# Sums and combine weights spread over partitions by way of DRAM, and multiplied on GpSimd

## The chip, the cores and the metric

The kernel runs on one core of one Trainium2 chip. The metric is the device time of one execution in microseconds. Beside it stands a profile, which is one execution recorded by the hardware: PE is TensorE's matmul, PEld its weight load, DVE is VectorE, ACT is ScalarE, POOL is GpSimd, SP is SyncE, which only issues DMAs here. POOL can issue DMAs too. Each engine carries out its instructions in the order in which they were built.

## What is computed

The reference is eight layers in a row on x of (4, 512, 128): four attentions and four feed-forward parts in turn, each followed by a sum with its input and a layernorm. Two of the eight are touched. The seventh is attention with 16 heads of 64 in groups of 16 tokens with relative positions; its softmax divides by a sum of exponentials. The eighth is a mixture of 16 experts with gates and a shared expert:

```python
sim = einsum('bid,bjd->bij', q, k) * scale + einsum('btd,tsd->bts', q, k2) * scale
attn = softmax(sim, axis=-1)
out = einsum('bij,bjd->bid', attn, v) + einsum('bts,tsd->btd', attn, v2)
return out @ Wo.T + bo
...
weights, idx = _gate(x, w_gate)
combine = (one_hot(idx, E) * weights[..., None]).sum(1)
g = silu(einsum('th,efh->tef', x, w1_e)); u = einsum('th,efh->tef', x, w3_e)
routed = einsum('tef,ehf,te->th', g * u, w2_e, combine)
shared = _swiglu(x, w1_s, w3_s, w2_s)
```

The 16 heads' outputs have to be multiplied by 1/sum, and the hidden values of every expert by that token's combine weight.

## The kernel before

The tokens are four blocks ("batches" b = 0 to 3) of 512; block b lives in SBUF as X[b]. Eight stage objects run in the order Causal, F0, Rel, F1, Alibi, F2, A3, F3. A stage is written as Python generators that yield between small steps; `K.step` (L160) advances all generators of a list by one step, so their instructions are interleaved. A framework beneath then orders the instructions of each engine by priority and by its own estimates, inserts the waits, and that order is fixed in the program. `K.turn` (L175) gives out the banks of PSUM tag "b" in turn.

**A3**, the seventh layer (class at L1128), works in 32 units, t = 0 to 31: unit t is heads 2un and 2un+1 of block b, with b, un = divmod(t, 8). `prep` (L1283) makes queries and keys of the next unit and spreads them with DMAs, most of them from SP, two for each unit from POOL (L1312, a3KT<-H). `score` (L1327) makes 128 x 512 scores, their minimum on DVE (L1349) and the exponential on ACT with its sum (L1350, into den). `turn` (L1355) transposes the probabilities (L219 within `tr`), copies them to SBUF on ACT (L1363), and writes a band of them to DRAM (a3dpw) which is read back as `at` (L1376). `tail` (L1378) has two POOL instructions (L1386, L1387, from `at` to a2), 16 matmuls with the values (L1393), two more (L1406, L1407) and a copy to OT (L1409): two heads' outputs, one head on partitions 0 to 63, the other on 64 to 127, 512 tokens along the free axis.

After four units `fin` (L1414) ends one half (hf) of the heads of a block. It takes the reciprocal of the sums (L1422), splits it into a high and a low float32r part (L1423, L1424), transposes 4 x (128 x 16), copies to a3lT (L1430), and for each of the four OT runs a matmul with a table of ones, a3sel (L1436), that puts head 2pr's row on partitions 0 to 63 and head 2pr+1's on 64 to 127; DVE multiplies OT by that PSUM bank (L1437). Then 16 matmuls with Wo (L1447), a sum on DVE (L1449) and, after the second half, the layernorm. `fin` starts in `run` (L1459) at the units with t % 4 == 1; the last one starts after the loop and runs beside the beginning of F3.

**F3**, the eighth layer (class at L2180), first splits its weights into high and low parts, 18 pieces of 128 columns: DVE casts f3wh (L1935), POOL subtracts to f3wl (L1936). Then a loop over 36 steps (four blocks, nine of each: the shared expert and eight pairs of experts): `hidden` (L2268) has six matmuls of 128 x 512 (L313 to L315 within `mm3`), silu on ACT (L2277) and a product on DVE (L2279) that gives h. `gate` (L2203), a generator that is started `ahead` = 7 steps before its block's first, makes the combine weights: transposes of X, four matmuls (L2212), sigmoid (L2215), small DVE operations, comparisons in `rank` whose part on POOL is L1924 (eqf3g over groups, four; eqf3e over experts, four), sums on DVE (L1926, L1928), normalisation (L2253), the split (L2256, L2257), transposes and the copy to f3cT (L2265). `weigh` (L2282), `lag` = 4 steps behind `hidden`, has a matmul with a table of ones, f3sel (L2287), which spreads two experts' weights over 64 partitions each, and the multiplication on DVE (L2288). `out` (L2290), two steps behind that, has four matmuls (L2297); after eight pairs and the shared expert, a sum (L2302) and the layernorm. There are `lag` + 5 = 9 buffers for h.

Of the kernel before, what the change touches and what calls it, by code (L numbers as in the profile page):

```python
# [7 lines left out]
F32 = mybir.dt.float32  # L8
# [31 lines left out]
class K:  # L40
# [249 lines left out]
    def split_w(self, pool, src, n, name, scales=(), tag=None, raw=("wraw", 1)):  # L290

        nc = self.nc
        h = pool.tile([P, n], F32R, name=name + "h", tag=(tag or name) + "h")
        l = pool.tile([P, n], F32R, name=name + "l", tag=(tag or name) + "l")

        def fill():
            for s in range(0, n, 512):
                e = min(n, s + 512)
                w = pool.tile([P, 512], F32, tag=raw[0], name=f"wraw{self.next()}", bufs=raw[1])
                self.late(nc.sync.dma_start(w[:, :e - s], src[:, s:e]))  # L300
                yield
                yield
                for a, b, f in scales:
                    if a <= s < b:
                        nc.vector.tensor_scalar(w[:, :e - s], w[:, :e - s], f, None, ALU.mult)
                nc.vector.tensor_copy(h[:, s:e], w[:, :e - s])
                nc.gpsimd.tensor_tensor(l[:, s:e], w[:, :e - s], h[:, s:e].bitcast(F32), ALU.subtract)
                yield
        return h, l, fill()

    def mm3(self, out, wh, wl, xh, xl):
        nc = self.nc
# [800 lines left out]
def a3_constants():  # L1113
    c = {}
    ql = np.arange(P)[:, None]
    x = np.arange(512)[None, :]
    c["c_right"] = (x >= ql).astype(np.float32)
    st = np.zeros((32, 2, 2, T), np.float32)
    for bk in range(32):
        st[bk, :, :, 16 * bk + 32:] = 1.0  # L1120
    c["c_step"] = st.reshape(64, 2, T)
    r = np.arange(16)[None, :]
    c["c_d16"] = (r < 16 - ql % 16).astype(np.float32)
    c["c_sel3"] = heads(8)
    return c


class A3:  # L1128
# [93 lines left out]
    def operands(self):  # L1222
        k, nc, d, pool, w = self.k, self.nc, self.k.d, self.pool, self.w
        w["right"] = pool.tile([P, 512], BF16, name="a3right")
        nc.gpsimd.dma_start(w["right"], d["c_right"])
        w["sel"] = self.more.tile([P, 4, P], F32R, name="a3sel")
        self.lT = k.rows16(self.more, "a3lT")
        nc.gpsimd.dma_start(w["sel"], d["c_sel3"])

        self.QT, self.KT, self.Q2, self.K2 = ([pool.tile([P, 2, T], F32R, name=f"a3{n}{i}") for i in range(2)] for n in ("QT", "KT", "Q2", "K2"))  # L1230
        for i in range(2):
            nc.gpsimd.dma_start(self.K2[i][64:P], d["c_step"])
# [145 lines left out]
    def tail(self, t):  # L1378
# [32 lines left out]
        self.left -= 1  # L1411
        yield

    def fin(self, b, hf, X):  # L1414

        k, nc, w, pool = self.k, self.nc, self.w, self.pool
        u = k.next()
        den = self.S[b][2]
# [40 lines left out]
    def run(self, Xs):  # L1459
# [720 lines left out]
class F3:  # L2180
# [22 lines left out]
    def gate(self, b, X):  # L2203
# [57 lines left out]
        for c in range(4):  # L2261
            k.tr(ps[:32, c * P:(c + 1) * P], c2[:, c, :])
        yield
        cT = self.cTs[b % 2]
        nc.scalar.copy(cT[:32], ps[:32, :])  # L2265
        self.cT[b] = cT

    def hidden(self, b, j):  # L2268
        k, nc, w, pool = self.k, self.nc, self.w, self.pool
# [12 lines left out]
    def weigh(self, b, j, h):  # L2282
        k, nc, w = self.k, self.nc, self.w
        while b not in self.cT:
            k.step(self.gs)
        cb = k.bank("t")
        nc.tensor.matmul(cb, w["sel"][:, j, :], self.cT[b], start=True, stop=True)  # L2287
        nc.vector.tensor_tensor(h, h, cb, ALU.mult)  # L2288
# [19 lines left out]
    def run(self, Xs):  # L2308
# [1 line left out]
        self.w["2"] = k.load(pool, d["f3_w2"], [P, 9, P], "f3w2")  # L2310
        self.w["sel"] = pool.tile([P, 8, P], F32R, name="f3sel")
        nc.gpsimd.dma_start(self.w["sel"], d["c_sel"])
        self.cTs = [k.rows16(pool, f"f3cT{i}") for i in range(2)]
# [94 lines left out]
```

## Time and profile before

| what | value |
|---|---|
| median of 3 runs | 2244.88 us (2244.24 to 2246.5) |
| the profiled execution's own time | 2239.62 us |
| its span | 2237.9 us |
| granted TensorE clock, mean | 0.965 |
| POOL busy | 501.9 us |
| DMA moved | 242.10 MB, of it POOL's queue (q0) 17.50 MB |
| A3, from its first units to its last | about 1550 to 2107 us |
| F3, from its first matmul of `hidden` to the end | 2112 to 2238 us |

The 2237.9 us of the span are what the views cut up; the profiled execution took 1.7 us more than its span. The page gives busy time for each engine, the span in 40 slices of 56 us, and groups of instructions by line. A row of a group reads: line, engine, operation, out<-in, count, busy us and mean ns of one, then the idle time of the engine before them and what ended most of it. Times in rows of the timeline are start and duration in us; "[5.21 <-DMA f3w...]" at the end of one is the engine's idle time before it and what ended that. Line numbers are those of the kernel before.

### The profile page before, as it was taken

To read this page: it belongs to the slowest core of one execution; us is meant where nothing else is said; L and a number is where in the kernel's file an instruction comes from. 1 tells how busy PE (TensorE), PEld (TensorE's weight loads), DVE (VectorE), ACT (ScalarE), POOL (GpSimd) and SP (SyncE) were. 2 spreads that over 40 slices of the span, in tenths; PEclk is the share of its full clock that TensorE was granted. 3 is DMA by queue.
4 is the path that set the end of the run, shared out by engine and by line. 5 is a ranking of instruction groups with operands and counts; after the bars stand their busy time and mean duration, and the time that the engine had idled before them with its cause. 6 is when DMAs were issued, how large, how long until landed. Compare 5 with 4: busy or idle time off the path is not lost.

```text
span 2237.9 us, 43122 instructions
## 1 busy us (share of the span) xinstructions
PE 2025.4 (91%) x14400; PEld 1477.7 (66%) x14400; DVE 1664.1 (74%) x5592; ACT 1333.5 (60%) x2983; POOL 501.9 (22%) x706
## 2 busy tenths in 40 slices
PE   7999788888888999999999999998999999999897
PEld 4666566676665667676887665786666566666676
DVE  5778689888878677873777785544777877778787
ACT  3566787787734656665333666333777777767632
POOL 3222212111212532433000322531111111111220
PEclk9999999999978999999999999999999999999999
DMA  5321322021433454421021420604888878888400
GB/s 171 106 77 35 109 50 57 6 48 27 116 113 108 130 175 125 127 65 57 15 67 48 116 78 15 219 17 112 214 209 198 211 192 193 199 194 211 99 5 15
DMA packets 264918, 242.10 MB, mean 108 GB/s; under 512 B 106352, under 2 KB 190618, under 8 KB 263866
## 3 DMA queue, kind: packets, MB, share of 16 engines
q1 hardware_dynamic: 259146, 221.33, 37.2%
q0 software_dynamic: 5232, 17.50, 3.3%
q8 instruction: 115, 1.88, 0.3%
q14 instruction: 105, 0.86, 0.1%
q10 hardware_dynamic: 320, 0.52, 0.1%
HBM read 103.82 MB, written 74.32 MB: 80 GB/s over the span
## 4 chain that ended last, share of the span: by engine, by line
PE 59%; DVE 17%; ACT 10%; DMA 7%; issue 4%; POOL 2%; SPq 1%; ACTq 0%; POOLq 0%; DVEq 0%
PE t L219 5%; PE s L2129 4%; PE o L1393 3%; PE o L744 3%; PE s L695 3%; PE t L728 3%; PE o L1032 3%; PE b L313 3%; PE b L219 3%; PE o L2025 3%; DMA a3dpw<-p 2%; PE s L313 2%; PE b L315 2%; PE b L314 2%; PE s L315 2%
## 5 line engine op out<-in xcount | busy, mean ns | idle before, releaser
L985 DVE CUSTOM_DVE_ANT_0 junk<-w,a1mask 128x640 bf16<-128x640 f32 x256 | 203.1, 818 | 67.3 <-PE w L983 65.4
L219 PE MATMUL t<-ident,p 128*128 128x128 f32 x1280 | 201.9, 279 | 23.8 <-ACT p L1350 15.7
L772 ACT ACTIVATE Pt<-t 128x384 f32<-128x384 f32 (+1 forms) x384 | 179.5, 528 | 65.8 <-PE t L728 54.4
L219 PEld LDWEIGHTS t<-ident,p 128*128 128x128 f32 x1280 | 151.7, 142 | 81.0 <-ACT p L1350 39.0
L1363 ACT COPY PT<-t 128x512 f32<-128x512 f32 x256 | 149.9, 596 | 71.9 <-PE t L219 70.9
L1059 ACT ACTIVATE Pt<-t 128x512 f32<-128x512 f32 x256 | 149.1, 597 | 72.7 <-PE t L1058 44.5
L1350 ACT ACTIVATE p<-s,nb 128x512 f32<-128x512 f32 x256 | 178.6, 702 | 12.8 <-DVE nb L1349 8.4
L1349 DVE TENSOR_REDUCE nb<-s 128x1 f32<-128x512 f32 x256 | 175.0, 687 | 2.6
L1368 DVE CUSTOM_DVE_ANT_0 jk<-p,a3right 128x496 bf16<-128x496 f32 (+3 forms) x256 | 125.0, 488 | 29.2 <-ACT p L1350 17.8
L697 DVE CUSTOM_DVE_ANT_0 junk<-s,a0mask 128x128 bf16<-128x128 f32 (+3 forms) x256 | 114.2, 485 | 43.4 <-PE s L695 42.4
L697 DVE CUSTOM_DVE_ANT_0 junk<-s,a2mask 128x128 bf16<-128x128 f32 (+3 forms) x256 | 114.9, 484 | 28.3 <-PE s L695 27.9
L781 POOL TENSOR_SCALAR_AFFINE_SELECT Pt<-Pt 128x512 f32<-128x512 f32 x112 | 69.9, 636 | 249.0 <-ACT Pt L772 248.9
L1344 PE MATMUL s<-a3KT,a3QT 128*128 128x512 f32 x256 | 118.9, 465 | 7.3 <-DMA a3K<-L 4.1
L1347 DVE TENSOR_TENSOR s<-s,W 128x160 f32<-128x160 f32 (+1 forms) x256 | 81.1, 318 | 56.1 <-PE s L1345 55.2
L1393 PE MATMUL o<-PT,V 128*64 128x512 f32 x512 | 116.9, 599 | 0.5 <-ACT PT L1363 0.5
L1707 ACT ACTIVATE p<-sm,nb 128x128 f32<-128x128 f32 x256 | 100.6, 396 | 24.8 <-DVE nb L1705 24.3
L1345 PE MATMUL s<-a3K,a3Q 128*128 128x512 f32 x256 | 102.7, 401 | 0.1
L1705 DVE CUSTOM_DVE_ANT_0 sm<-s,band,rn 128x128 f32<-128x128 f32 x256 | 78.3, 344 | 26.5 <-PE s L1692 19.3
L1056 PE MATMUL t<-a1Q,a1K 128*128 128x512 f32 (+3 forms) x256 | 92.4, 366 | 6.2 <-ACT Pt L1059 3.6
L695 PE MATMUL s<-a0K,a0Q 128*128 128x256 f32 (+2 forms) x256 | 83.6, 387 | 14.0 <-DVE mx L697 6.8
L982 PE MATMUL w<-a1K,a1Q 128*128 128x256 f32 (+2 forms) x192 | 83.8, 437 | 9.3 <-DVE mx L985 8.3
L2012 ACT ACTIVATE sl<-s 128x512 f32<-128x512 f32 x64 | 38.0, 598 | 91.0 <-PE s L315 85.6
(494 smaller groups left out, 5812.7 us busy)
## 6 DMA issues: line engine op xcount, KB each, us to landing
W<-a3dsk SPq DMA_DIRECT2D x32, 640.0 KB
a1Q<-a1iq SPq DMA_DIRECT2D x32, 512.0 KB
a3dpw<-p SPq DMA_DIRECT2D x64, 160.0 KB
a3dpw<-p SPq DMA_DIRECT2D x64, 144.0 KB
a1K<-a1ik SPq DMA_DIRECT2D x64, 128.0 KB
a3Q<-a3dim SPq DMA_DIRECT2D x32, 256.0 KB
a3KT<-H POOLq DMA_DIRECT2D x64, 128.0 KB, 4.4
a3KT<-H SPq DMA_DIRECT2D x64, 128.0 KB
```

Of the source, the lines that this page charges most:

```text
L219: return self.nc.tensor.matmul(out.bitcast(x.dtype), x, i[:n, :n], is_transpose=True, start=start, stop=stop)
L695: self.scored = nc.tensor.matmul(s[:, :nm], self.qof(0, t, i)[:, qc * P:(qc + 1) * P], Ks[:, i, :nm], start=True, stop=True).ins
L697: nc.vector.tensor_tensor_reduce(junk[:, :n], s[:, :n], k.mask[:, 512 - n:512], 1.0, NEG, ALU.add, ALU.max, mx[:, qc, i:i + 1])
L772: ready = nc.scalar.activation(Pt[:, i, z:], s[:, z:], AF.Exp, scale=sc).ins
L985: nc.vector.tensor_tensor_reduce(junk, s.rearrange("p a n -> p (a n)")[:, T - n:T + m], k.mask[:, T - n:T + m], 1.0, NEG, ALU.add, ALU.max ...
L1059: nc.scalar.activation(Pt[:, i, :T], s, AF.Exp, scale=sc)
L1344: nc.tensor.matmul(s, QT[:, e, qs], KT[:, e, :], start=True, stop=False)
L1349: nc.vector.tensor_reduce(nb, s, AX.X, ALU.min)
L1350: nc.scalar.activation(p[:, e, :], s, AF.Exp, bias=nb, scale=-1.0, accum_out=den[:, qc, 2 * un + e:2 * un + e + 1])
L1363: self.copied[t] = nc.scalar.copy(PT[e][:, :, qc * P:qc * P + P], tb.rearrange("p (c n) -> p c n", n=P)).ins
L1368: nc.vector.tensor_tensor_reduce(jk[:, :nn], p[:, e, x0:], w["right"][:, :nn], 1.0, 0.0, ALU.mult, ALU.add, at[:, e, qc, 31:32])
L1393: m = nc.tensor.matmul(o[64 * e:64 * e + 64, :], V[:, kc, h * 64:h * 64 + 64], PT[e][:, kc, :], start=(kc == 0), stop=False)
```

## The change

In A3 the reciprocals are no longer split and spread by a matmul. A new generator `sums` takes the reciprocal, transposes it in float32, copies the 8 rows to SBUF and writes them to a DRAM tile with a DMA from POOL (`rows_out`). It starts three items into the fourth of four units (t % 4 == 0; after the last unit at its first item), so ahead of `fin`. `fin` reads two rows for each OT back with two DMAs from POOL, each of which sends one row of 512 values to 64 partitions (`rows_in`), and POOL multiplies OT by that. Two buffers alternate: one of the stage's own, and the one that the tile a3z had. `fin`'s matmuls with the table and its products on DVE go, as do the table a3sel and the tile a3lT.

In F3 block 0 stays as it was. For blocks 1 to 3 the gate transposes the weights in float32, copies 16 rows to SBUF, writes them to DRAM from POOL, and reads them back into two tiles of 128 x 4 x 512, each with two DMAs of 64 partitions; POOL multiplies h by a slice of these. The matmul with f3sel and DVE's multiplication go for these blocks.

```diff
+    def rows_out(self, rows, name):
+        n = rows.shape[0]
+        d = self.dr.tile([n, T], F32, tag=f"rows{n}", name=name, bufs=2)
+        self.nc.gpsimd.dma_start(d, rows)
+        return d
+
+    def rows_in(self, dst, d):
+        n = d.shape[0] // 2
+        for e in range(2):
+            ap = [[0, 64], [2 * T, n], [1, T]] if n > 1 else [[0, 64], [1, T]]
+            self.nc.gpsimd.dma_start(dst[64 * e:64 * e + 64], bass.AP(tensor=d.tensor, offset=d.offset + e * T, ap=ap))
...
@@ A3.operands @@
-        w["sel"] = self.more.tile([P, 4, P], F32R, name="a3sel")
-        self.lT = k.rows16(self.more, "a3lT")
-        nc.gpsimd.dma_start(w["sel"], d["c_sel3"])
...
+    def sums(self, b, hf):
+        k, nc = self.k, self.nc
+        u = k.next()
+        rd = self.more.tile([P, 4, 8], F32, tag="rd", name=f"rd{u}", bufs=2)
+        nc.vector.reciprocal(rd, self.S[b][2][:, :, 8 * hf:8 * hf + 8])
+        yield
+        ps = k.bank("b")
+        for c in range(4):
+            k.tr(ps[:8, c * P:(c + 1) * P], rd[:, c, :])
+        yield
+        lr = self.more.tile([8, T], F32, tag="lrow", name=f"lrow{u}", bufs=1)
+        nc.scalar.copy(lr, ps[:8, :])
+        yield
+        self.S["R", b, hf] = k.rows_out(lr, f"a3rows{u}")
+
     def fin(self, b, hf, X):
...
-        lr = self.more.tile([P, 4, 16], F32R, tag="lr", name=f"lr{u}", bufs=1)
-        rd = self.more.tile([P, 4, 8], F32, tag="rd", name=f"rd{u}", bufs=2)
-        nc.vector.reciprocal(rd, den[:, :, 8 * hf:8 * hf + 8])
-        nc.vector.tensor_copy(lr[:, :, 0:8], rd)
-        nc.vector.tensor_tensor(lr[:, :, 8:16], rd, lr[:, :, 0:8].bitcast(F32), ALU.subtract)
-        yield from wait()
-        ps = k.bank("b")
-        for c in range(4):
-            k.tr(ps[:16, c * P:(c + 1) * P], lr[:, c, :])
-        lT = self.lT
-        nc.scalar.copy(lT[:16], ps[:16, :])
+        rows, rbs = self.S["R", b, hf], []
+
+        def load(pr):
+            rbs.append((self.early, self.more)[pr % 2].tile([P, T], F32, tag=("a3z", "rb")[pr % 2], name=f"rb{u}{pr}", bufs=1))
+            k.rows_in(rbs[-1], rows[2 * pr:2 * pr + 2])
+
+        load(0)
+        load(1)
         yield
         for pr in range(4):
-            yield from wait()
-            ps = k.bank("b")
             OT = self.S["O", b, 4 * hf + pr]
-            nc.tensor.matmul(ps, w["sel"][:, pr, :], lT, start=True, stop=True)
-            nc.vector.tensor_tensor(OT, OT, ps, ALU.mult)
+            nc.gpsimd.tensor_tensor(OT, OT, rbs.pop(0), ALU.mult)
+            if pr < 2:
+                load(pr + 2)
             yield
...
@@ A3.run @@
+            if t >= 4 and t % 4 == 0:
+                sums = self.sums(*divmod((t - 4) // 4, 2))
...
+                if j == (self.la if t < n else 0) and t >= 4 and t % 4 == 0:
+                    gs.append(sums)
...
@@ F3.gate @@
+        if b:
+            yield
+            yield from k.turn()
+            ps = k.bank()
+            for c in range(4):
+                k.tr(ps[:16, c * P:(c + 1) * P], cw[:, c, :])
+            yield
+            cr = pool.tile([16, T], F32, tag="cr", name=f"cr{u}", bufs=2)
+            nc.scalar.copy(cr, ps[:16, :])
+            rows, cb = k.rows_out(cr, f"f3rows{b}"), []
+            for i in range(2):
+                cb.append(pool.tile([P, 4, T], F32, tag="cb", name=f"cb{u}{i}", bufs=3))
+                k.rows_in(cb[i], rows[8 * i:8 * i + 8])
+            self.cT[b] = cb
+            return
...
@@ F3.weigh @@
+        if b:
+            nc.gpsimd.tensor_tensor(h, h, self.cT[b][j // 4][:, j % 4, :], ALU.mult)
+            return
         cb = k.bank("t")
         nc.tensor.matmul(cb, w["sel"][:, j, :], self.cT[b], start=True, stop=True)
         nc.vector.tensor_tensor(h, h, cb, ALU.mult)
```

More of the change, by code (lines that the diff above doesn't have):

```diff
@@ L1123, in a3_constants @@
     c["c_d16"] = (r < 16 - ql % 16).astype(np.float32)
-    c["c_sel3"] = heads(8)
     return c
@@ L1417, in fin @@
         u = k.next()
-        den = self.S[b][2]
         wait = k.turn if b == NB - 1 and hf else lambda: ()
-        lr = self.more.tile([P, 4, 16], F32R, tag="lr", name=f"lr{u}", bufs=1)
-        rd = self.more.tile([P, 4, 8], F32, tag="rd", name=f"rd{u}", bufs=2)
-        nc.vector.reciprocal(rd, den[:, :, 8 * hf:8 * hf + 8])
-        nc.vector.tensor_copy(lr[:, :, 0:8], rd)
-        nc.vector.tensor_tensor(lr[:, :, 8:16], rd, lr[:, :, 0:8].bitcast(F32), ALU.subtract)
-        yield from wait()
-        ps = k.bank("b")
-        for c in range(4):
-            k.tr(ps[:16, c * P:(c + 1) * P], lr[:, c, :])
-        lT = self.lT
-        nc.scalar.copy(lT[:16], ps[:16, :])
+        rows, rbs = self.S["R", b, hf], []
[4 more added lines that the diff above has]
+        load(1)
         yield
         for pr in range(4):
-            yield from wait()
-            ps = k.bank("b")
             OT = self.S["O", b, 4 * hf + pr]
-            nc.tensor.matmul(ps, w["sel"][:, pr, :], lT, start=True, stop=True)
-            nc.vector.tensor_tensor(OT, OT, ps, ALU.mult)
+            nc.gpsimd.tensor_tensor(OT, OT, rbs.pop(0), ALU.mult)
+            if pr < 2:
+                load(pr + 2)
             yield
@@ L2263, in gate @@
         yield
-        cT = self.cTs[b % 2]
-        nc.scalar.copy(cT[:32], ps[:32, :])
-        self.cT[b] = cT
+        nc.scalar.copy(self.cT0[:32], ps[:32, :])
+        self.cT[b] = self.cT0
     def hidden(self, b, j):
@@ L2312, in run @@
         nc.gpsimd.dma_start(self.w["sel"], d["c_sel"])
-        self.cTs = [k.rows16(pool, f"f3cT{i}") for i in range(2)]
+        self.cT0 = k.rows16(pool, "f3cT0")
         gs = self.gs = [self.gate(0, Xs[0])]
```

## The prediction

> **What bounds the kernel.** First the page: busy times and slices.
>
> ```profile
> PE 2025.4 (91%) x14400; PEld 1477.7 (66%) x14400; DVE 1664.1 (74%) x5592; ACT 1333.5 (60%) x2983; POOL 501.9 (22%) x706
> ...
> DMA  5321322021433454421021420604888878888400
> ```
>
> POOL is nearly free over the whole span, and the DMA engines are fullest in slices 29 to 37, where A3 runs. F3 comes after, with the DMA engines empty. The two stages have different limits, so each is read by itself.
>
> A3, 1600 to 2100 us, who waited for whom (total us, times, longest):
>
> ```profile
> POOL a L1386 <- DMA at<-a3dpw: 159.1, 16, 16.7
> POOL a3KT L1312 <- ACT H L1307: 145.7, 28, 9.2
> ...
> PE s L1344 <- DMA a3K<-L: 4.1, 3, 1.7
> ```
>
> POOL stands idle; PE hardly waits for DMA. PE's share of windows of 100 us there is 89 to 96%, and dense rows start 0.23 us apart for a 512-column matmul. But the chain of waits runs through transfers too: in 1720 to 1860 "DMA a3dpw<-p" alone holds 11.9% of it, in 1860 to 2085 two transfers and SP's issues about 17%. So A3 is mostly PE, with DMA close behind at 84% of its engines.
>
> F3, cut where each batch's combine weights are ready (end of the copy at L2265: 2140.4, 2165.2, 2190.9, 2216.9):
>
> ```profile
> core 0: us, PE busy (x) PEld busy (x) DVE busy (x) ACT busy (x) POOL busy (x), PEclk, DMA share, GB/s
> 2113.30:2140.60 27.30, 22.90 (x120) 18.45 (x119) 24.32 (x84) 9.15 (x16) 8.29 (x17) 0.94 0.00 1
> 2140.60:2165.40 24.80, 23.52 (x146) 19.59 (x145) 20.48 (x66) 8.88 (x15) 5.53 (x8) 1.00 0.01 2
> 2165.40:2191.10 25.70, 24.52 (x150) 20.74 (x150) 22.48 (x81) 9.64 (x15) 5.43 (x8) 1.00 0.04 11
> 2191.10:2217.00 25.90, 24.31 (x145) 20.04 (x144) 22.16 (x81) 8.63 (x13) 5.45 (x8) 1.00 0.04 11
> 2217.00:2229.10 12.10, 10.64 (x72) 9.16 (x72) 8.45 (x24) 0.00 (x0) 0.00 (x0) 1.00 0.08 22
> ```
>
> PE's starts sum to only some 20 us a round (54 of 0.23, 36 of 0.11, 8 of 0.23, small ones); its busy column is filled by modelled ends. The round is one gate: PE issues the next batch's L2212 right behind the transposes of this one's weights, and then sigmoid, DVE, POOL's L1924, DVE, transposes and copy follow one another. In the round from 2190.9: group ranks leave POOL 7.3 us in, expert ranks start 4.4 later and take 4.6, DVE needs 8.0 more, transposes and copy 1.7. The last row is the tail: 12.2 us from the copy to the last sum's reader.
>
> **The change, part by part**, against the profiled execution (2239.62 us, span 2237.9; the runs' median of 2244.88 lies 5.3 above).
>
> *A3, removed.* 32 matmuls with the table (L1436): 32 x 0.23 = 7.4 us of PE; PE's idle time before them is 8.6 more at most (3.8 + 3.2 + 1.6 by that line's rows). On DVE 32 multiplications of 0.68 and 8 x (0.17 + 0.18) for the split, 24.6 us. Transposes and ACT's copy stay. Bounds: 0 (something else ends the waits) to -16.0. I take 70% of the PE time and half of the idle time: -9.5.
>
> *A3, added.* 72 POOL issues of 0.52 and 32 multiplications of 1.28 (rows below): 78 us spread over stretches where POOL idles, so nothing by themselves. The transfers are 8.4 MB more. At the stage's own 197 GB/s that is 42.6 us if DMA decides, nothing if hidden: bounds 0 and +42.6. With DMA and SP holding about 15% of the chain I take 0.15 x 42.6 = +6.4. POOL's order puts two to four a3KT issues (L1312) behind a multiplication that waits for its rows: write and read back, some 10 us once in four units. In the trace a3KT is issued more than half a unit before its unit (1674.65, 1686.64, 1702.28, a unit being 16 us), so I take nothing; without that cover it is up to 4 us, seven times. A3 in sum: -3.
>
> The trace shows all queues together at 84%, POOL's own with 6.1%, and not what happens when POOL's grows. The Trainium skill ("DMA: Bandwidth & Descriptors", section "Issuing engines are not separate DMA queues") says that DMAs of any issuing engine share the same 16 engines and interleave. By it the idle POOL queue buys no room: with the full +42.6 in place of +6.4 the forecast would be 36 us later.
>
> *Into F3.* The last four outputs of A3 now go through POOL, ahead of the work that opens F3. Before:
>
> ```profile
> 2107.34 0.56 POOL L2312 DMA_DIRECT2D f3sel<-in_c_sel_dram  x1
> 2107.89 1.00 POOL L272 MEMSET f3cT<- 128x512 f32 x2
> 2109.16 2.59 POOL L1936 TENSOR_TENSOR f3wl<-f3w,f3wh 128x128 fp32r<-128x128 f32 x6 [0.26 <-DVE f3wh L1935]
> ```
>
> After, POOL's order is: rows out, two a2 instructions, four rb issues, f3sel, two multiplications, four issues, memset, the third multiplication, six f3wl, four eqf3g with four f3wl between, the fourth multiplication, eight f3wl, four eqf3e. PE's order puts the matmuls with OT before the first one with f3wl. From 2107.4: four issues to 2109.6; rows landed 2.5 us on, products to 2113.6; issues to 2115.8; third product 2118.7; six f3wl at 0.43 to 2121.3; ranks and f3wl to 2124.1; fourth product 2125.4; eight f3wl 2128.9; four eqf3e of 1.14 to 2133.5. They ended at 2128.4 before. So +5; bounds +3 (DVE, 24.3 of 27.3 busy there, was late anyway) to +9 (the delay of the first f3wl).
>
> *The rounds.* Batch 0 keeps its matmul, so the first round stays. The rows with prices:
>
> ```profile
> L1441 POOL TENSOR_TENSOR r<-X,a3bo 128x512 f32<-128x512 f32 x4 | 5.1, 1276 | 11.9 <-DVE X L375 11.9
> L1924 POOL TENSOR_TENSOR eqf3e<-eqf3e,f3tri 128x256 f32<-128x256 f32 x16 | 17.1, 1092 | 18.9 <-DVE eqf3e L1923 13.4 <-issue 4.2 <-DVE rs L345 0.4
> L2288 DVE TENSOR_TENSOR h<-h,t x32: 669/682/690, 2141.9 to 2227.2; 128x512 f32<-128x512 f32 x32
> DMA to landing us min/median/max: 3.8/3.8/3.8
> ```
>
> The last is f3sel: 512 KB on quiet engines, of which 256 KB of output moved at about 300 GB/s in the same state; fixed part about 2.5. From the end of the copy: rows issued and landed +2.6; cb waits for that, four issues of 0.55; the first megabyte lands 5.5 after its first issue, +8.1 (bound above: f0v's 5.5 for 512 KB, twice, +13.6; below +7). POOL then runs in its written order: three multiplications mixed with eqf3g, four more, one eqf3e, the eighth, three eqf3e: 8 x 1.28 + 4 x 0.25 + 4 x 1.14 = 15.8, to +23.9. Before, eqf3e ended at +16.3. DVE's 8.0 afterwards shrinks by about three L2288 (2.0) and the dropped split (0.4): 5.6, then 1.7: a round of 31.2 against 25.9. As DVE also loses 5.5 us elsewhere in the round I take 30.5, +4.7 for each of the rounds 2 and 3: +9.4 (bounds +4 and +20).
>
> *The end.* Copy, +8.1, eight multiplications 10.2, last four matmuls and the wait 0.7: 19.0 instead of 12.2: +6.8 (bounds +5 and +12).
>
> DVE and POOL in one another's way: in the first gate DVE's L344, L346 and L349 take 0.73, 0.70 and 0.70 beside eqf3e instead of 0.16, and end with it; in later gates eqf3e runs beside DVE's 0.42 us rows unstretched. The Trainium skill ("Advanced Engine Details and Errata", section "VectorE Performance Modes") says that DVE's second SBUF port is shared with GpSimd, so two-port DVE instructions and POOL's block each other. Eight waits of 0.55 would fit in the 4 us in which eqf3e queues behind multiplications; by the page the sum may rise some 3 us, by the rows it does not.
>
> Sum: -3 + 5 + 9.4 + 6.8 = +18.2, 2257.8 for the profiled execution and 2263 for the median.
>
> **The rivals.** *Faster:* DVE decides the rounds (22.2 of 25.9 us busy). Freed of eight multiplications a round loses 5.5, and latency hides behind the nine h buffers: -11, A3 -14 with nothing lost to DMA, end +6.8: 2227. It decides when POOL reaches eqf3e before DVE has it ready, that is when the seventh multiplication ends less than 11.7 us into the round; with rows landing at +8.1 it ends near +18. Chance 0.13. *Level:* A3 gains its whole 16 and the three F3 terms sit at their lower bounds, 12: -4, about 2242 to 2247. Chance 0.13. *DMA or POOL decides A3:* the transfers come in lumps of 1 MB (5.3 us at 197 GB/s) in one unit of four, whose 16 us are 84% full already; a3Q, a3K and a3KT are late and A3 loses 30: 2296. For it the chain's transfers, against it PE's 7 us of waiting in all. Chance 0.14. *It does not do what it says:* excluded, the built order has 56 table matmuls fewer.
>
> **Numbers.** Forecast 0.60, its own range 2250 to 2280. Range for all 2241 to 2288: left out are the faster rival and the upper part of the DMA one. Faster by over 0.2% (about what a measurement of this kernel can tell from no change) 0.13, within 0.13, slower 0.74.
>
> **What would show it.** Right: copies of the weights about 30 us apart in rounds 2 and 3; eqf3e idle-free behind multiplications; some 19 us from the last copy to L2302; the first f3wl some 9 us later than in the row above; A3 within a few us of before. Wrong: rounds under 26 us, or a3KT and a3Q among PE's longest waits.

## The result and the profile after

The changed kernel takes 2322.0 us (median of 6, 2317.47 to 2331.26) against 2244.57 (median of 6): 1.0353 times, with a 95% interval of 1.0325 to 1.0381. It is slower, as predicted, but by 77 us, not 18, and outside the range. The profiled execution took 2317.61 us, its span is 2315.9, 78.0 longer than before. The page of the changed kernel, busy times and the DMA row of the slices:

```profile
PE 2038.6 (88%) x14344; PEld 1488.5 (64%) x14344; DVE 1665.6 (72%) x5514; ACT 1333.8 (58%) x2983; POOL 616.3 (27%) x846
...
DMA  5321411012326444212204206038899887887123
```

56 table matmuls are gone, POOL has 114 us more, and the span is longer although no engine but POOL is busy for a larger share of it. So most of the time went into waits. Where, is read from four marks: the first and the last copy to OT, the copies of the weights in F3, and the sum after the last block. Starts in both traces, differences worked out from them:

| stretch | before | after | difference | forecast |
|---|---|---|---|---|
| start to first copy to OT | 1586.6 | 1587.4 | +0.8 | 0 |
| A3: first to last copy to OT | 522.9 | 569.9 | +47.0 | -3 |
| last copy to OT to first copy of weights | 30.3 | 38.1 | +7.8 | +5 |
| first to second copy | 24.8 | 24.1 | -0.7 | 0 |
| second to third, third to fourth copy | 25.7, 26.0 | 32.4, 33.6 | +14.3 | +9.4 |
| last copy to last sum | 12.8 | 21.6 | +8.8 | +6.8 |

A3 alone holds 50 of the 60 us that the forecast lacks. Two rows of windows tell in what form: A3 before, then A3 after, each from its first copy to OT to just after its last.

```profile
core 0: us, PE busy (x) PEld busy (x) DVE busy (x) ACT busy (x) POOL busy (x), PEclk, DMA share, GB/s
1586.00:2110.00 524.00, 492.37 (x2753) 326.76 (x2752) 406.57 (x1179) 384.59 (x906) 72.06 (x128) 0.99 0.83 197
```

```profile
1587.00:2158.00 571.00, 503.23 (x2727) 336.28 (x2725) 401.34 (x1144) 385.33 (x909) 143.17 (x219) 0.95 0.82 193
```

PE is idle for 571.00 - 503.23 = 67.77 us where it was for 31.63: +36.1. And with fewer matmuls its busy time grows by 10.9, because the granted clock falls from 0.99 to 0.95. The DMA share is what it was. Before, PE's largest wait in A3 (1590 to 2110 us) was this, and none ahead of the matmuls with Wo (L1447) is in that answer:

```profile
PE t L219 <- ACT p L1350: 14.8, 23, 2.1
```

Who waited for whom in 1600 to 2150 us, after:

```profile
POOL a L1396 <- DMA at<-a3dpw: 132.1, 14, 13.4
POOL a3KT L1322 <- ACT H L1317: 107.1, 21, 8.5
...
POOL OT L1456 <- DMA rb<-a3rows: 47.1, 16, 4.9
PEld b L1468 <- POOL OT L1456: 40.7, 15, 6.9
PE b L1468 <- POOL OT L1456: 37.4, 13, 6.7
```

L1468 are the matmuls with Wo (L1447 before). They wait for POOL's multiplication, and that waits for the loaded rows; PE and its weight load show the same waits, so they are not added up. One half, on POOL:

```profile
1628.47 0.54 POOL L315 DMA_DIRECT2D a3rows<-lrow  x1
1631.16 2.07 POOL L323 DMA_DIRECT2D rb<-a3rows  x4 [2.15 <-DMA a3rows<-lrow]
1638.14 1.27 POOL L1456 TENSOR_TENSOR OT<-OT,rb 128x512 f32<-128x512 f32 x1 [4.91 <-DMA rb<-a3rows]
1639.71 1.07 POOL L323 DMA_DIRECT2D rb<-a3rows  x2 [0.30 <-POOL OT L1456]
...
1641.82 1.33 POOL L1456 TENSOR_TENSOR OT<-OT,rb 128x512 f32<-128x512 f32 x1
1644.63 1.28 POOL L1456 TENSOR_TENSOR OT<-OT,rb 128x512 f32<-128x512 f32 x1 [1.49 <-DMA rb<-a3rows]
1645.85 1.09 POOL L323 DMA_DIRECT2D rb<-a3rows  x2
...
1651.82 1.26 POOL L1456 TENSOR_TENSOR OT<-OT,rb 128x512 f32<-128x512 f32 x1 [3.68 <-DMA rb<-a3rows]
```

From the rows' DMA to the end of the fourth product 24.6 us pass: write 2.4, load, product, and with two buffers a second turn of load and product, of which the last load stands behind the third product. The transposes of the reciprocals had ended at 1626.51, so from there the chain is 26.6 us long; in the other halves it is 22 to 26. PE had 16.7 us of other work between these transposes and its first matmul with Wo (15 to 18 in seven of the eight halves, 7 in the last). It came to the matmul with the fourth OT at 1646.45, stood for 6.68 us, and went on at half speed:

```profile
1646.50:1649.00 2.50, 0.00 (x0) 0.00 (x0) 0.29 (x1) 0.00 (x0) 1.56 (x3) 1.00 1.09 248
1649.00:1653.00 4.00, 0.00 (x0) 0.00 (x0) 0.68 (x1) 1.72 (x4) 1.18 (x1) 0.56 1.04 230
1653.00:1656.00 3.00, 2.87 (x12) 2.68 (x12) 1.18 (x4) 0.00 (x0) 0.08 (x1) 0.50 0.05 14
1656.00:1660.00 4.00, 4.00 (x34) 3.78 (x32) 1.83 (x9) 3.78 (x10) 0.00 (x0) 0.96 0.00 0
```

The column before DMA's share is the granted clock: 1.00 until some 3 us into the wait, then 0.50 until some 3 us after PE is busy again. In the third row DMA is empty too: SP stood 7.4 us for ACT's p before it could issue the next transfers of a3dpw.

F3, windows cut at the end of the copies (the rows that answer to those shown of before):

```profile
2196.00:2220.10 24.10, 22.36 (x138) 19.19 (x137) 21.02 (x55) 9.21 (x14) 4.16 (x8) 1.00 0.00 1
2220.10:2252.50 32.40, 25.92 (x147) 22.16 (x145) 26.65 (x72) 9.75 (x16) 17.33 (x21) 0.89 0.34 75
2252.50:2286.10 33.60, 26.52 (x140) 21.98 (x139) 25.89 (x71) 8.74 (x13) 17.03 (x21) 0.85 0.33 72
2286.10:2307.10 21.00, 14.48 (x89) 13.03 (x88) 6.48 (x27) 1.80 (x3) 12.85 (x13) 0.84 0.52 115
```

Block 0 keeps its matmul, and its round is as before; the others are 7 and 8 us longer, with the clock at 0.89 and 0.85. The last row is the end.

### The profile page after: what moved, and what is told of

It is laid out like the page before. It is cut to its first block, busy times and chain, and to the rows that moved or that the text cites. A ratio compares the mean times of both kernels' runs of the same rounds, so it can differ in the third digit from the quotient of the medians.

```text
span 2315.9 us, 43157 instructions
## 1 busy us (share of the span) xinstructions
PE 2038.6 (88%) x14344; PEld 1488.5 (64%) x14344; DVE 1665.6 (72%) x5514; ACT 1333.8 (58%) x2983; POOL 616.3 (27%) x846
## 4 chain that ended last, share of the span: by engine, by line
PE 51%; DVE 17%; DMA 12%; ACT 10%; issue 5%; POOL 4%; SPq 1%; POOLq 0%; ACTq 0%; DVEq 0%
PE s L2154 4%; PE t L219 3%; DMA rb<-a3rows 3%; PE s L709 3%; PE o L758 3%; PE t L742 3%; PE o L1046 3%; PE b L219 2%; PE o L2050 2%; PE o L1403 2%; PE b L327 2%; PE s L327 2%; PE s L329 2%; PE s L328 2%; DVE junk L999 2%
## 5 line engine op out<-in xcount | busy, mean ns | idle before, releaser
L219 PE MATMUL t<-ident,p 128*128 128x128 f32 x1280 | 206.0, 283 | 18.4 <-ACT p L1360 10.2
L219 PEld LDWEIGHTS t<-ident,p 128*128 128x128 f32 x1280 | 156.6, 144 | 83.5 <-ACT p L1360 36.8
L1360 ACT ACTIVATE p<-s,nb 128x512 f32<-128x512 f32 x256 | 178.1, 700 | 20.6 <-DVE nb L1359 12.5
L1378 DVE CUSTOM_DVE_ANT_0 jk<-p,a3right 128x496 bf16<-128x496 f32 (+3 forms) x256 | 135.5, 529 | 29.6 <-ACT p L1360 18.7
L711 DVE CUSTOM_DVE_ANT_0 junk<-s,a0mask 128x128 bf16<-128x128 f32 (+3 forms) x256 | 114.1, 484 | 42.6 <-PE s L709 41.7
L1468 PE MATMUL b<-a3wo,OT 128*128 128x128 f32 x256 | 49.0, 330 | 47.9 <-POOL OT L1456 46.8
```

The source lines that it names most:

```text
L219: return self.nc.tensor.matmul(out.bitcast(x.dtype), x, i[:n, :n], is_transpose=True, start=start, stop=stop)
L711: nc.vector.tensor_tensor_reduce(junk[:, :n], s[:, :n], k.mask[:, 512 - n:512], 1.0, NEG, ALU.add, ALU.max, mx[:, qc, i:i + 1])
L1360: nc.scalar.activation(p[:, e, :], s, AF.Exp, bias=nb, scale=-1.0, accum_out=den[:, qc, 2 * un + e:2 * un + e + 1])
L1378: nc.vector.tensor_tensor_reduce(jk[:, :nn], p[:, e, x0:], w["right"][:, :nn], 1.0, 0.0, ALU.mult, ALU.add, at[:, e, qc, 31:32])
```

## The experiments

The theories: **W**, PE's written order puts the matmuls with Wo where the old path was through and the new one is not, so PE waits; **T**, my rival on record, the traffic of the loads; **P** or **M**, POOL's order and its multiplications. For F3: **D**, the trip through DRAM, against M. In the table A3 is the time from the first to the last copy to OT; the next column goes from there to the first copy of weights; rounds are first to last copy of weights, all three; the end is last copy to last sum. Ratios are those to the kernel before, run on the same chip, with 95% intervals.

| kernel | ratio | A3 | into F3 | rounds | end |
|---|---|---|---|---|---|
| before | 1 | 522.9 | 30.3 | 76.5 | 12.8 |
| after | 1.0353 (1.0325 to 1.0381) | 569.9 | 38.1 | 90.1 | 21.6 |
| e1_a3_part | 1.0265 (1.0224 to 1.0306) | 576.1 | 38.9 | 78.1 | 14.2 |
| e2_f3_part | 1.0092 (1.0063 to 1.0121) | 522.6 | 28.4 | 92.0 | 21.8 |
| e3_rows_unread | 1.0151 (1.0115 to 1.0188) | 558.7 | 35.0 | 76.4 | 12.9 |
| e4_wo_later | 1.0083 (1.0051 to 1.0115) | 531.6 | 37.3 | 78.7 | 12.5 |
| e5_wo_later_sp | 1.0267 (1.0235 to 1.0299) | 578.1 | 38.3 | 78.6 | 12.5 |
| e6_a3_dve | 1.0206 (1.0166 to 1.0247) | 562.6 | 36.1 | 77.4 | 12.6 |
| e7_f3_dve | 1.0120 (1.0081 to 1.0158) | 519.8 | 28.3 | 90.3 | 22.6 |
| e8_f3_bank_pool | 1.0049 (1.0030 to 1.0067) | 524.1 | 30.6 | 77.1 | 23.2 |
| e9_rows_unread_order | 1.0168 (1.0137 to 1.0200) | 545.1 | 39.4 | 77.8 | 12.8 |
| e10_wo_later_act | 1.0118 (1.0087 to 1.0150) | 540.5 | 37.2 | 78.6 | 12.5 |
| e11_spread | 1.0074 (1.0053 to 1.0095) | 526.0 | 38.0 | 75.8 | 12.8 |
| e12_loads_only | 1.0130 (1.0094 to 1.0165) | 551.0 | 34.4 | 76.1 | 12.8 |
| e13_small_loads | 1.0132 (1.0099 to 1.0165) | 549.1 | 38.1 | 76.2 | 12.8 |
| e14_small_loads_only | 0.9989 (0.9970 to 1.0008) | 522.7 | 33.1 | 76.1 | 12.7 |
| e15_spread_last | 1.0028 (1.0011 to 1.0044) | 530.8 | 30.6 | 76.2 | 12.8 |

Each stretch is from one profiled execution, each ratio from all runs. The single executions scatter: the stretches of F3, which e3 to e6 and e9 to e15 leave as before, differ by up to 3 us in the rounds.

**The two parts by themselves.** The edit of each is the diff of that stage alone. The experiments on A3 that follow start from e1, with F3 as before.

> Only the part in A3 is changed; F3 is as before. Theory W (waiting): PE's written order puts the matmuls with Wo (L1468) 14 to 16 us of PE work behind the transposes of the reciprocals, while the new chain (copy, rows out, two loads, multiplication, two more loads, multiplications) takes some 27 us; PE stands idle for the rest, about 6 us in each of eight halves. Theory T (traffic): the 8.4 MB more make A3's own transfers late. Theory P (POOL): POOL's waits and multiplications, in its one order, hold back a, a3KT and DVE. All three put the whole 48 us of A3 and 7 us until F3's first gate is through into this kernel: before + 54, about 2299 us. If the two parts make each other worse, less: 2270 to 2290. They differ in the rows: W has 45 to 50 us of PE's idle time before L1468 with POOL's multiplication as its end, T has it at L1354 and L1386 with a DMA as its end, P has it at L1416 or L1354 with POOL's a or a3KT.

> Only the part in F3 is changed; A3 is as before. From the two traces: rounds 2 and 3 longer by 6.7 and 7.6 us, the end by 8.8, the first round shorter by 0.7: before + 22, about 2267 us. My forecast had +16 for these three terms (2261). If F3's loss were a consequence of A3's late end it would be below +10.

2307.5 and 2266.1 us: 2.65% and 0.92%, whose sum is the change's 3.53% within the intervals. A3's part was some 5 us worse than expected; PE waits 46.6 us there for POOL's multiplications, the last half taken in, as W had it. The cause of A3's loss lies in A3, that of F3's in F3.

**Take the wait away, keep the traffic.**

```diff
-            nc.gpsimd.tensor_tensor(OT, OT, rbs.pop(0), ALU.mult)
-            if pr < 2:
-                load(pr + 2)
+            ov = OT.rearrange("p (c n) -> p c n", c=4)
+            nc.gpsimd.tensor_tensor(ov, ov, w["bo"][:, None, :].to_broadcast([P, 4, P]), ALU.mult)
+            if pr > 1:
+                load(pr)
```

> The part in A3 alone, with all of its DMAs (rows out, eight loads for each half) and POOL's 32 multiplications, but these multiply by the bias row a3bo that is in SBUF, so nothing reads the loaded rows, and the third and fourth pair of loads are issued after the third and fourth multiplication; the division by the sums is left out. PE's order of L1468 is the same (14 to 16 us behind the transposes). Theory W: no wait is left before L1468 but the few us in which POOL's loads wait for the rows; A3 about as before less the 32 table matmuls, and a few us until F3's first gate: before - 8 to + 5, 2237 to 2250 us. Theory T: all the traffic is there, so before + 40 to + 54, 2285 to 2299 us. Theory P: POOL's work and its waits for the rows are there, so half or more of the loss stays, 2270 to 2290 us.

2281.2 us: in P's range, above W's and below T's. PE waits for no multiplication any more, but POOL now stood 97 us for ACT's copies to OT: without the loads to wait for, the framework had moved the multiplications forward, ahead of a and a3KT. So POOL's order is not that of the change, and this run does not tell the theories apart; e9 below repeats it with POOL's order held.

**Move the matmuls with Wo back.**

```diff
         r = self.r
+        for _ in range(8):
+            yield
         yield from wait()
         y = k.bank("b")
```

> The part in A3 alone, with eight more yields in fin ahead of the matmuls with Wo. In the built order they stand 27 to 30 us of PE work behind the transposes of the reciprocals in five of the eight halves (14 to 16 without the yields), 17 to 21 in two, and as before at 4.5 in the last, which runs after the loop. The chain takes some 27. Theory W: the five halves lose nothing, two lose some 3, the last 4 to 7 with the 7 until F3's gate: before + 12 to + 20, 2257 to 2265 us, unless the five buffers for OT, now held longer, make a new wait at L1416 or L1403. Theories T and P: traffic and POOL's work are unchanged, so before + 45 to + 54, 2290 to 2299 us.

2264.2 us: all of the traffic, all of POOL's work, and 43 us less than e1. That is W, and neither T nor P alone. PE now has 20 to 38 us of work between the transposes and these matmuls in seven halves, and its waits for the multiplications are down to 5.8 us, in the last half:

```profile
PE b L1470 <- POOL OT L1456: 5.8, 2, 3.7
```

A3 and the way into F3 are still 9 and 7 us longer than before. What is left are waits of another kind, the longest 5.0, 4.1, 3.8 and 3.5 us, ended by ACT or by a3KT.

**Who issues a3KT.** I took those waits for POOL's late a3KT. In e4 the issue goes from POOL to SP (e5), or to ACT (e10):

```diff
-(nc.gpsimd if s is H and i and e else nc.scalar if t == 0 and e else nc.sync)
+(nc.scalar if t == 0 and e else nc.sync)                      # e5
+(nc.scalar if s is H and i and e or t == 0 and e else nc.sync) # e10
```

> As e4_wo_later (the part in A3 with the matmuls with Wo moved back), and the two transfers of every unit that POOL issues, a3KT<-H (L1322), are issued by SP instead, as the other six of that kind are. In the rows of e4_wo_later PE's long waits are no longer at the matmuls with Wo: they are 3.8, 5.0, 3.5, 4.1 and 2.8 us long and end with ACT or with the transfer a3KT<-H. Theory P2: what is left of A3's loss comes from a3KT<-H standing in POOL's order behind loads that wait for rows or buffers; until it has landed, the buffer of H is not free, ACT waits and PE with it. Then these waits go, A3 is as long as before or 5 us shorter, and the time falls by 8 to 20 us to 2245 to 2256. If the traffic itself is what is left (theory T), the waits stay, with other transfers as their end: 2260 to 2268. If SP's own order is the tighter one, they move to a3Q or a3dpw and the time rises.

> As e4_wo_later (2264), with the two transfers a3KT<-H of every unit issued by ACT instead of POOL; SP, which lost 40 us by taking them in e5_wo_later_sp, keeps its own. Theory P2 (a3KT behind POOL's waiting loads holds the buffer of H and so ACT and PE): the waits of 3 to 5 us go, 2245 to 2256. If the traffic is what is left: 2260 to 2268. If 64 more issues on ACT, 70% busy in A3, cost more than they free: above 2268.

2304.6 and 2269.8 us; e10 is just above 2268, where the issues would cost ACT more than they free. P2 finds no support: issued by ACT, the transfers leave waits of the same size (PE 5.07, 4.98, 4.48 and 4.14 us, ended by ACT's p twice, by POOL's a and by a3K). With 64 more issues on SP 40 us are lost, and PE then waits for L (22.9 us in 21 waits) and for a, whose transfers are SP's. So both runs moved the issue to a busier engine; how a3KT would do without POOL's loads ahead of it and without this price was not shown.

**Multiply on DVE.** In e1, `nc.gpsimd.tensor_tensor(OT, OT, rbs.pop(0), ALU.mult)` becomes `nc.vector...`.

> The part in A3 alone (as e1_a3_part), but DVE does the 32 multiplications (SBUF by SBUF) and POOL only issues the DMAs; the matmuls with Wo stand 14 to 16 us behind the transposes as in e1_a3_part. Theory W: the round trip through DRAM in two steps of two buffers is most of the chain, POOL's multiplication is 4 x 1.27 of some 27 us, DVE's would be 4 x 0.68 and have DVE's queue ahead of it: PE's idle time before L1468 falls by a third at most, and the time by 5 to 20 us against e1_a3_part: 2288 to 2303. If POOL's multiplication were the cause (theory P), the time is within 10 us of before: 2245 to 2258. If the traffic is (theory T), it is that of e1_a3_part, 2303 to 2312.

2288.7 us, the fast edge of W's range. PE's waits for the multiplications fall from 46.6 us to 18.9, the last half taken in, which is more than the third that W allowed. Part of the rest has moved to DVE's order: ACT's p waits 39.7 us for the minima that stand behind a multiplication that waits for its rows. 44 of e1's 59 us stay: the trip has to be waited for on whichever engine, and DVE's multiplications wait 44.9 us for their loads.

**F3: trip without POOL's multiplication, and the reverse.** e7 is e2 with `nc.vector` for `nc.gpsimd` in `weigh`; e8 is before with

```diff
         nc.tensor.matmul(cb, w["sel"][:, j, :], self.cT[b], start=True, stop=True)
+        if b:
+            cs = pool.tile([P, T], F32, tag="cs", name=f"cs{k.next()}", bufs=3)
+            nc.scalar.copy(cs, cb)
+            nc.gpsimd.tensor_tensor(h, h, cs, ALU.mult)
+            return
         nc.vector.tensor_tensor(h, h, cb, ALU.mult)
```

> The part in F3 alone (as e2_f3_part, which took 33.9 us for each of rounds 2 and 3 and 21.8 from the last copy to the last sum), but DVE does the multiplications of h by the loaded weights. The trip through DRAM stays (copy, rows out, four loads, 10.8 us from the copy to the first product). Theory D (the trip): most of the loss is these 10.8 us ahead of the gate's next steps; DVE now waits for them in its own order, rounds 30 to 34, the end 10.8 + 8 x 0.69 + 1.5 = 17.8: before + 13 to + 21, 2258 to 2269. Theory M (POOL's multiplications, which hold eqf3e and, by the rows, stretch DVE's small operations from 0.17 to 0.22 up to 0.9 to 1.4 us): rounds 26 to 28 and the end 17.8, before + 5 to + 10, 2250 to 2258.

> F3 without the trip, A3 as before: the matmul with f3sel spreads the weights as before, ACT copies the PSUM bank to SBUF (0.6 us, 24 times), and POOL multiplies h by that. POOL's 24 multiplications and their place in its order are those of e2_f3_part. Theory D: without the trip the rounds are 26 to 28 us and the end about 13 to 15 (eight multiplications of 1.27 behind the first copy), before + 3 to + 7, 2248 to 2254. Theory M: eqf3e still queues behind eight multiplications and DVE's small operations are stretched beside them, rounds 29 to 32, before + 9 to + 16, 2254 to 2263.

2270.0 and 2256.9 us, just above D's range and, for e8, in M's. The rounds give a clean answer, D: with the trip and no multiplication on POOL they take 90.3, with POOL's multiplications and no trip 77.1, before 76.5. The end does not, and it carries e8's time out of D's range: 22.6 and 23.2, each above what I expected. In e7 the two megabytes landed one after the other (first product 11.8 us after the copy's end, fifth 16.6), and PE then had 64 matmuls left. In e8 POOL stood for ACT's copies, 13.2 us in five waits of up to 5.0, as ACT makes them in one order with the silus.

**Take the wait away, hold POOL's order.** As e3, with `k.behind(m.ins, self.last.ins)` for each multiplication, an order without a wait behind the loads just issued.

> As e3_rows_unread (the part in A3 alone, all DMAs and multiplications kept, the multiplications by the bias row a3bo, so nothing reads the loaded rows and the division is left out), but each multiplication is bound to its place behind the loads in POOL's order, as in the change. In e3_rows_unread they had moved ahead, to wait for ACT's copy of OT (97 us in 16 waits) with a and a3KT behind them. PE's order is as in the change. If that move was what cost e3_rows_unread its 33 us, theory W alone is left: before - 5 to + 8, 2240 to 2253 us. If loads that wait on POOL for rows and buffers, with a and a3KT behind them, cost as much by themselves (theory P), it stays at 2265 to 2285, and the rows show PE behind ACT's dh and the H buffers, as in e3_rows_unread. Theory T: 2265 to 2299, with transfers of SP's queue late.

2279.1 us, in the ranges of P and T and 26 us above W's, which I had expected to be left alone. A3 is 545.1: of e1's loss of 53 us in A3, 31 go with the wait and 22 stay. PE now waits for ACT's p (30.6 us in 28 waits), and that for DVE's minima (38.0 in 31, the longest 4.8).

**What the rest is: loads, multiplications, both, neither.** e12 is e9 without the multiplications; e13 is e9 with `dst[64 * e:64 * e + 1]` in the loads, one partition instead of 64; e14 has the small loads and no multiplication.

> As e9_rows_unread_order (2279, before + 37) without POOL's 32 multiplications: rows out and all loads stay, nothing multiplies OT, so the division is left out. Theory T (the loads' traffic, and ACT's wait for the buffer of H behind it): most of the 37 stays, 2265 to 2280 us. Theory M (multiplications on POOL, DVE longer beside them): the time falls to 2240 to 2255.

> As e9_rows_unread_order, but every load fills one partition instead of 64: 2 KB instead of 128 KB, in the same places of POOL's order; nothing reads them, POOL multiplies by the bias row, and the division is left out. Theory T: most of the 37 goes, 2240 to 2252 us. Theory M: most stays, 2265 to 2280.

> As e13_small_loads without the multiplications: rows out and loads of one partition, nothing divides. What A3 would be if all that replaces the table matmuls were free: before less 32 x 0.23 us of PE, less its idle time there: 2230 to 2240 us for theories T and M alike. If it is above 2250, the loss lies in neither of them but in what the new order of PE and POOL is without them.

2274.2, 2275.9 and 2244.5 us: e12 as T had it, e13 as M had it, e14 above its range by 4.5. A3 takes 551.0, 549.1 and 522.7. Loads alone cost A3 28 us, multiplications alone 26, both (e9) 22, neither nothing. These are single executions, and e12's was the slowest of its four; by the ratios the whole kernels are +29, +30, +38 and -2 us. So T and M are each enough for a loss, and together they cost less than their sum. Each has its row. With the loads, ACT waits for a buffer for dh, which by the code is one of H's two, and PE waits with it (5.86, 4.98 and 4.13 us, where blocks 1 to 3 open):

```profile
1656.44 0.58 ACT L1374 COPY PT<-t 128x512 f32<-128x512 f32 x1
1663.16 0.58 ACT L1262 CAST dh<-b 16x512 fp32r<-16x512 f32 x1 [6.14 <-DMA a3dpw<-p]
```

The row names a3dpw<-p as what came last; where another block opens it is a3Q<-H (4.2 us), one of the transfers that hold H. In e15 below, where dh has a buffer of its own, ACT's dh waits for no transfer.

With the multiplications, DVE stands still while POOL multiplies several times in a row. e13, DVE and then POOL:

```profile
1711.65 0.28 DVE L1379 CUSTOM_DVE_ANT_0 jk<-p,a3right 128x112 bf16<-128x112 f32 x1
...
1712.32 4.78 DVE L1379 CUSTOM_DVE_ANT_0 jk<-p,a3right 128x112 bf16<-128x112 f32 x1 [0.39 <-ACT p L1361]
```

```profile
1712.29 3.76 POOL L1458 TENSOR_TENSOR OT<-OT,a3bo 128x512 f32<-128x512 f32 x3
1715.99 1.03 POOL L323 DMA_DIRECT2D rb<-a3rows  x2
1717.04 1.30 POOL L1458 TENSOR_TENSOR OT<-OT,a3bo 128x512 f32<-128x512 f32 x1
```

The same instruction takes 0.28 us alone and 4.78 beside three multiplications and the two DMA issues behind them. Of e13's seven such rows four end 0.13 to 0.14 us behind the run, three only with those issues. In the change itself the multiplications stand singly or in twos, mostly with loads between: the longest of this line is 1.95 us there, 2.98 in e1, 5.49 in e13 and 1.13 before; its mean is 0.49 us before, 0.54 in the change and 0.65 in e13. So a good part of M's 26 us is the experiment's own. T's 28 may be so too: in the first half e12 issues its eight loads within 10.8 us, the change within 15.2. What made up e9's 22 in the change itself, with the waits in place, was not shown.

e14 also prices the whole gain: with the replacement nearly free, A3 is as long as before, though 32 matmuls are gone.

**What can be kept.** e11 spreads the steps of `fin`; e15 adds a buffer of its own for dh (the one of lrow) and the old path for the last half.

```diff
         for pr in range(4):
+            for _ in range(0 if last else (4, 0, 3, 0)[pr]):
+                yield
...
         r = self.r
+        for _ in range(0 if last else 6):
+            yield
```

> The part in A3 alone, with yields in fin between the first loads and the first multiplication (4), between the second and the third multiplication (3) and ahead of the matmuls with Wo (6), not in the last half: those matmuls then stand 32 to 35 us behind the transposes in six of the eight halves. Theory W: PE no longer waits for the multiplications, and POOL waits less for loads; what is left is the last half and the way into F3, about 10: 2250 to 2258, a little under e4_wo_later's 2264. If five buffers for OT are too few for that distance, ACT's copies to OT wait for PE's matmuls with Wo, and PE for the bank of o: 2264 to 2285.

> A version meant to keep what can be kept: as e11_spread (2261), with the tile dh of each even half in a buffer of its own instead of one of H's two, and the last half by the table matmul as before, F3 as before. It computes the whole reference. In e11_spread's rows two of PE's waits, 4.5 and 4.0 us, have ACT's dh and its buffer in the chain, and the last half and the way into F3 cost some 7. With both gone: 2243 to 2252 us, that is about before; below 2240 only if the 32 x 0.23 us of PE are gained in full. If T or M costs more than these waits it stays at 2255 to 2262.

2260.9 us for e11, a little above its range, with A3 at 526.0 in the profiled run, which was 9 us faster than the median: with all loads and all multiplications in place, only 3 us above before; 2251.5 for e15, which is the best of these versions that divide by the sums, and still 0.1 to 0.4% above before. The last half by matmul brings "into F3" back to 30.6.

## Why the prediction was wrong

That the kernel gets slower was forecast, and F3's part alone would have made it so, by the mechanism foreseen (e2, 0.92%). But 47 of the 78 us come from A3, which was forecast to gain 3.

**A3, removed (-9.5): wrong, 0.** e14 has 32 matmuls less and A3 at 522.7 against 522.9. I took 70% of PE's time as gained because PE is 89 to 96% busy; the chain of waits that I quoted, with its transfers, was the better witness. Where the 7 us went was not shown.

**A3, added: the step that failed.** The text says of POOL's issues and multiplications: "78 us spread over stretches where POOL idles, so nothing by themselves". POOL's busy time was rightly nothing. What they make late I looked for at a3KT, as the row behind the waiting instruction on POOL, and did not follow on to the product's own reader. That reader is PE's L1447 (L1468 after), 15 to 18 us of PE's work behind the transposes in seven of the eight halves, with a chain of 22 to 27 us in front. The prediction had the pieces for it: written in F3's part as 2.5 for the rows, a load, 1.28 a product, and the built order had the place. Inside A3 37.4 us of waiting, and a clock that halves in the longer waits, are +36.1 of PE's idle time and, with some 6 us fewer matmuls, 10.9 more of its busy time: the +47. e4, which moves only this reader back, returns 43 of e1's 59 us. The level rival, with A3's whole 16 gained, falls by the same rows.

**The traffic (+6.4): within its bounds, its price in the change open.** e12 against e14 measures 28 us in A3 for the loads by themselves; with all of them and PE's reader moved back, A3 is 9 above before in e4 and 3 in e11. By the page's rule that DMAs of all issuers share 16 engines (the Trainium skill, "DMA: Bandwidth & Descriptors", section "Issuing engines are not separate DMA queues") the prediction had named +42.6 as the full price; the direction of e12 agrees. The place that the rival named (a3Q, a3K late) was wrong; in e12 the price shows at the buffer that ACT needs. The loads are also the longest part of the chain that PE waits for: in 1620 to 1665 us they are 35.2% of what ended last, and one of 128 KB took 4.6 us (median), where f3sel's 512 KB landed in 3.8 before.

**a3KT behind POOL's waits (0): right, as far as was shown.** PE's waits for a3K sum to 4.5 us in A3, it has none for a3KT among its listed waits, and e5 and e10 did not gain by moving the issue. Neither sign named for being wrong came, rounds under 26 us or a3KT and a3Q among PE's longest waits: the loss came from a place that the prediction had not named.

**Into F3 (+5): +7.8.** The order was as foretold, and the last half goes through the same chain; one row more than I had: DVE's gtf3g, 0.21 us before (median), takes 4.99 beside POOL's run of f3wl.

```profile
2171.74 4.99 DVE L1951 TENSOR_TENSOR gtf3g<-gtf3g,eqf3g 128x64 f32<-128x64 f32 x1 [7.29 <-POOL eqf3g L1949]
```

```profile
2172.09 1.25 POOL L1456 TENSOR_TENSOR OT<-OT,rb 128x512 f32<-128x512 f32 x1
2173.31 3.35 POOL L1961 TENSOR_TENSOR f3wl<-f3w,f3wh 128x128 fp32r<-128x128 f32 x8
```

I had weighed the rule on the shared port (the Trainium skill, "Advanced Engine Details and Errata", section "VectorE Performance Modes") at up to 3 us and set it to nothing by the rows of later gates. The rows of e13 and this one agree with the page in that DVE and POOL block each other; that these are two-port instructions no row shows. The wait is not for one POOL instruction but for a whole run of them: this one ends at 2176.73, the run at 2176.66.

**The rounds (+9.4): +14.3, right in mechanism.** The round from 2252.5, POOL:

```profile
2252.76 0.55 POOL L315 DMA_DIRECT2D f3rows<-cr  x1 [7.02 <-ACT cr L2288]
2254.89 2.47 POOL L323 DMA_DIRECT2D cb<-f3rows  x4 [1.59 <-DMA f3rows<-cr]
...
2263.31 1.29 POOL L2327 TENSOR_TENSOR h<-h,cb 128x512 f32<-128x512 f32 x1 [5.69 <-DMA cb<-f3rows]
...
2266.31 6.17 POOL L2327 TENSOR_TENSOR h<-h,cb 128x512 f32<-128x512 f32 x5
...
2278.09 0.73 POOL L1949 TENSOR_TENSOR eqf3e<-eqf3e,f3tri 128x256 f32<-128x256 f32 x1 [0.36 <-DVE eqf3e L1948]
```

From the copy to the first product 10.8 us, forecast 8.1: the first megabyte landed 8.2 us after its first issue, not 5.5. From there to the end of eqf3e 15.5 us, forecast 15.8. To the end of the next copy 7.2, forecast 7.3. The mis-sized term is the landing: the prediction took 300 GB/s, and these loads move at 206 to 238 GB/s in the slices that they fill, two megabytes at a time. (At 300 GB/s its row leaves 2.05 us as the fixed part and not the 2.5 written there; its 5.5 goes by 2.05.) And the 0.7 that I took off for DVE did not come. e7 and e8 show that the trip decides here, not POOL's row of multiplications, which I had as its equal.

**The end (+6.8): +8.8.** From the copy's end to the first product 10.0 instead of 8.1, eight products 9.9 (10.2), from there to the sum 1.2 (0.7), with the granted clock at 0.57 from 2294 to 2302 us.

**The rival "DVE decides the rounds"** falls: DVE is freed of eight multiplications a round and the rounds are longer.

## What to carry to other kernels

A product that moves to an idle engine may cost little there, but its reader stands at a place in another engine's fixed order that was chosen for the old path: take the new chain from source to reader, buffer turns included, and compare it with the work that the built order leaves in between (here 22 to 27 against 15 to 18 us in seven halves, and against 7 in the last). A stall of PE can cost more than its length: here PE went on at half clock after the longer ones. And a busy share of 90% does not mean that removed work is gained. Before weighing traffic in bytes, look for the buffer whose release waits for it.

## What was new about the hardware

- PE's granted clock went to 0.50 1.9 to 3.0 us into a wait, by rows of 1 us at 1649, 1803 and 1878, and came back 3.2 to 4.5 us after PE was busy again. Each of these waits had another of 1.0 to 1.6 us that ended 0.5 to 1.9 us ahead of it. The Trainium skill ("TensorE: Matmul & The Clock Gate", Part 1) gives about 3.4 us for both, in free-running windows; the way back agrees; the way down came earlier here, but no row shows it for a wait that stands alone.
- A DVE instruction that meets POOL's multiplication can wait for a run of them: 0.28 to 4.78 us (e13), 0.21 before to 4.99 (after). What counts is mostly the run: with single multiplications and pairs, and mostly with DMA issues between them, the same line took at most 1.95 us in the change and 2.98 in e1.
- A row written to DRAM and read back to 64 partitions: 2.4 us for the write (1.8 to 3.8) and 4.6 for the read of 128 KB (2.8 to 6.8) in A3; in F3, with no other stage's transfers beside them, 1.9 for the write and 8.1 (4.9 to 11.2) for 512 KB, four such reads in flight.
